# Feed-forward output tile 0 kept on chip, with its norm, residual sum and maxima formed inside the feed-forward stage

## The chip, the core and the metric

The kernel runs on one core of a Trainium2 chip. The core has five engines with queues of their own: TensorE (PE, matmuls; its weight loads are shown as PEld), VectorE (DVE), ScalarE (ACT), GpSimd (POOL) and SyncE (SP, which here only issues transfers). Each queue runs its instructions in order; semaphores order the queues against each other. Data live in SBUF (128 partitions), matmul results in PSUM, and everything larger in HBM behind 16 DMA engines. The metric is device time of one launch in microseconds (us), lower is better. Before the change it is 4735.76 us, the median of three runs (4731.34 to 4744.84).

## The reference

Four residual blocks work on one image tensor `x` of 4 batches, 384 channels and 64 x 64 pixels, each behind a norm over 32 groups of 12 channels (`_gn`). The change lies at the border of the last two: the end of block 2 (a gated channel mixer) and the beginning of block 3 (a 7x7 depthwise convolution with generated kernels).

```python
# block 2, its end (tok: tokens formed before; gate: one number per batch)
h1 = _gelu(_bn(_pw(tok, cm_w1), cm_g1, cm_b1))     # 384 -> 768 channels
h2 = _bn(_pw(h1, cm_w2), cm_g2, cm_b2)             # 768 -> 384; _bn: mean and variance over batches and pixels
ch = tok + h2
return gate * ch + (1.0 - gate) * x

# block 3, on _gn(x)
x_avg = x.mean(axis=(2, 3)); x_max = x.max(axis=(2, 3))
x_w = gelu(x_avg @ w_avg.T + b_avg + x_max @ w_max.T + b_max)
x_w = x_w[:, :, None] * w_mix[None, :, :]
kern = gamma * (xr * Nx) + beta          # xr: x_w as b x c x 7 x 7, Nx: its norm over the mean norm
out = depthwise_conv_7x7(x, kern)

# the whole: x = x + block(_gn(x)), for each of the four
```

## The kernel before

Channels lie on partitions in three tiles of 128, j = 0, 1, 2 (`NJ`), in an order that puts each group's channels together as far as possible; the rest of the groups is spread over the three tiles, so a group's mean (`of_groups`, one small matmul and a few copies) needs all three tiles. A batch of one tile is 128 x 4096 float32, 2 MB; work on it is done in quarters of 1024 pixels.

**The feed-forward stage, `phase_ef`.** Its first half (L1640 to L1692) makes the hidden layer and, beside it, everything of the block's output that doesn't need h2: `wx`, in HBM, with its sums per channel (`sums`). It uses the start of the strip buffer `self.z_` as a spare tile. The second half (L1702 to L1731) runs over batch b and quarter i. It loads a 3 MB block of the hidden layer (`f_h`, two buffers), applies a Gelu to each of its six parts (L1708), and for each output tile j forms two 512-pixel products of six matmuls each (L1720) into one of four PSUM tiles `h2_m`. ScalarE copies each to SBUF (L1727), VectorE takes its statistics (L1728), and a transfer from GpSimd's queue writes it to `self.h2` in HBM (L1729). A float32 matmul appears as two matmul instructions in the profile. After the last product, `over_batches` and `bn_scale_shift` (L1732) turn the statistics into a scale and shift, and L1736 to L1745 into `gh` and `g0` (h2's scale and shift, with the gate), `mean2` (the mean of the block's output, called x2) and `neg2`, for all three tiles.

**The convolution stage, `phase_g`.** It begins with loads of constants and gate weights, `group_means()` (which gives the group means `gm` and from them the offset `s_b`), and then, batch after batch for tile 0:

- `x2_of(0, b)`: x2 = wx + gh * h2 + g0, in quarters. h2 is loaded from HBM (L1963), scaled on GpSimd (L1965), added on VectorE (L1966), squared with a sum on ScalarE (L1976) and searched for its maximum on VectorE (L1977). The whole goes to HBM (L1979). wx of batches 0 to 2 was loaded ahead into the three tiles of `gx_tile` (`x2_ahead`); that of batch 3 and of all later calls is loaded when a tile is free again (L1957).
- `to_strips(0, b, x)`: subtracts the group mean (L1993), transposes on TensorE (L2003) and copies into the strip buffer as `z[:, channel, row pair, batch]`, on VectorE (L2008) or ScalarE (L2010). A strip copy so writes scattered single elements all over the buffer. `x2_of` of one batch and `to_strips` of the batch before alternate.

Then `conv7` runs over channels: a band matrix `toep` on VectorE or GpSimd (L2036) and products with the strips (L2049), for tile 0 first. Meanwhile `x2_of(1, b)` and `x2_of(2, b)` are worked off, a piece at a time; after these, `factors()` forms the gates, which need sums and maxima of all three tiles. `half_strips` and `boxes` serve the later tiles.

The order of the program isn't the order on the queues: a planner fixes each queue's order when the program is built, from the order in which operations are written, what each needs, and `tc.high_priority()`, which asks for an earlier place.

Of the kernel before, what the change touches and what calls it, by code (L numbers as in the profile page):

```python
# [21 lines left out]
F32 = mybir.dt.float32  # L22
# [6 lines left out]
NJ = 3  # L29
# [252 lines left out]
class _Builder:  # L282
# [1301 lines left out]
    def phase_ef(self, strips):  # L1584
        tc, nc = self.tc, self.nc
        with ExitStack() as ctx:
# [113 lines left out]
            st2 = cp.tile([P, NJ, B * 8, 6], F32, tag="h2_st", name="h2_st")  # L1700
            mvb = cp.tile([P, NJ, B, 2], F32, tag="h2_mvb", name="h2_mvb")
            for b in range(B):  # L1702
                for i in range(4):
                    blk = slice(i * 1024, (i + 1) * 1024)
                    h = hp.tile([P, 6, 1024], F32, tag="h", name="f_h")
                    nc.sync.dma_start(h, self.hidden[b][:, :, blk].rearrange("o p n -> p o n"))
                    for o in range(6):
                        last = nc.scalar.activation(  # L1708
                            h[:, o, :], h[:, o, :], AF.Gelu, bias=c1[:, o : o + 1], scale=a1[:, o : o + 1]
                        )  # L1710
                    if b == B - 1 and i == 3:
                        self.ln_exp(last)
                    if b == B - 1 and 0 < i:
                        nc.sync.dma_start(self.x2_ahead[i - 1], self.wx[i - 1][:, 0])
                    for j in range(NJ):
                        out = io.tile([P, 1024], F32, tag="x", name="f_h2")
                        for v in range(2):
                            m = self.pm("h2_m")
                            for o in range(6):
                                nc.tensor.matmul(  # L1720
                                    m,
                                    lhsT=w2[:, o, j * P : (j + 1) * P],
                                    rhs=h[:, o, v * 512 : (v + 1) * 512],
                                    start=o == 0,
                                    stop=o == 5,
                                )
                            nc.scalar.copy(out[:, v * 512 : (v + 1) * 512], m)  # L1727
                            nc.vector.bn_stats(st2[:, j, 8 * b + 2 * i + v, :], out[:, v * 512 : (v + 1) * 512])  # L1728
                        nc.gpsimd.dma_start(self.h2[b][:, j, blk], out)  # L1729
                for j in range(NJ):  # L1730
                    nc.vector.bn_aggr(mvb[:, j, b], st2[:, j, 8 * b : 8 * b + 8].rearrange("p a b -> p (a b)"))  # L1731
            a2, c2 = self.bn_scale_shift("bn_h2", *self.over_batches("h2", mvb), self.vec("cm_g2"), self.vec("cm_b2"))  # L1732


            self.mean2, self.neg2 = self.coef("mean2"), self.coef("neg2")
            nc.vector.tensor_reduce(self.mean2, sums, AX.X, ALU.add)  # L1736
            for j in range(NJ):
                nc.vector.tensor_scalar(self.gh[:, j, :], self.gate, a2[:, j : j + 1], None, ALU.mult)
                nc.vector.tensor_scalar(self.g0[:, j, :], self.gate, c2[:, j : j + 1], None, ALU.mult)
                m = self.mean2[:, j, :]  # L1740
                nc.vector.scalar_tensor_tensor(m, m, 1.0 / N, self.g0[:, j, :], ALU.mult, ALU.add)
                part = self.sm([P, B], "h2_part")
                nc.vector.tensor_mul(part, self.gh[:, j, :], mvb[:, j, :, 0])
                nc.vector.tensor_add(m, m, part)
                nc.vector.tensor_scalar(self.neg2[:, j, :], m, -1.0, None, ALU.mult)  # L1745


    def phase_g(self):
# [8 lines left out]
        with ExitStack() as ctx:  # L1757
# [31 lines left out]
            self.x2_var, self.x2_max = (cp.tile([P, NJ, B, 4], F32, tag=k, name=k) for k in ("x2_var", "x2_max"))  # L1789


            self.z = self.z_[:, 0 : P * 136].rearrange("p (c k b) -> p c k b", k=34, b=B)
            nc.gpsimd.memset(self.z_[:, P * 136 :], 0.0)
            nc.gpsimd.memset(self.z[:, :, 0], 0.0)
            self.group_means()
            behind = iter(())
            for b in range(B):
                for x in self.x2_of(0, b):
                    next(behind, None)
                for _ in behind:  # L1800
                    pass
                behind = self.to_strips(0, b, x)
            for _ in behind:
                pass
# [144 lines left out]
    def x2_of(self, j, b):  # L1949
# [3 lines left out]
        if self.x2_ahead:  # L1953
            x = self.x2_ahead.pop(0)
        else:
            x = self.gx_tile("x2")
            nc.sync.dma_start(x, self.wx[b][:, j])  # L1957
        for q in range(4):
            sl = slice(q * 1024, (q + 1) * 1024)

            pool, tag = (self.gt_p, "rest") if j == 0 and q % 2 else (self.gw_p, "w7")
            h = pool.tile([P, 1024], F32, tag=tag, name="g_h2", bufs=3)
            nc.sync.dma_start(h, self.h2[b][:, j, sl])  # L1963
            if j == 0:
                nc.gpsimd.tensor_scalar(h, h, at(self.gh), at(self.g0), ALU.mult, ALU.add)  # L1965
                nc.vector.tensor_add(x[:, sl], x[:, sl], h)  # L1966
            else:
                for v in range(2):
                    m = self.pm("x2_m")
# [221 lines left out]
```

## Time and profile before

| what | value |
|---|---|
| median of three runs | 4735.76 us |
| the profiled execution | 4751.16 us, its span 4749.0 us |
| PE, busy | 4376.2 us, 92% of the span |
| DVE, busy | 2851.0 us, 60% |
| ACT, busy | 1958.1 us, 41% |
| POOL, busy | 845.5 us, 18% |
| DMA | 745.55 MB, mean 157 GB/s |
| second half of the feed-forward stage | 3533 to 4031 us of the span |
| between its last product and the first 7x7 product | 4031 to 4110 us |
| first tile's 7x7 products, to the gates | 4110 to about 4330 us |

The profile is of one execution. Busy time of PE is counted from start to modelled end of matmuls that overlap, so a busy PE need not be at its peak. The row of slices gives busy shares in tenths of 40 equal slices of 118.7 us; slices 34 and 35 hold the border of the two stages:

```profile
PE   7899999999999999998978999699999999578889
DVE  6766566655556455555777888655521111767788
PEclk9999999999999999998989999799999999698999
DMA  4301211121112111112328999766764442997787
```

PEclk is the clock that TensorE was granted, in tenths of full speed.

### The profile page before, as it was taken

To read this page: it belongs to the slowest core of one execution; us is meant where nothing else is said; L and a number is where in the kernel's file an instruction comes from. 1 tells how busy PE (TensorE), PEld (TensorE's weight loads), DVE (VectorE), ACT (ScalarE), POOL (GpSimd) and SP (SyncE) were. 2 spreads that over 40 slices of the span, in tenths; PEclk is the share of its full clock that TensorE was granted. 3 is DMA by queue.
4 is the path that set the end of the run, shared out by engine and by line. 5 is a ranking of instruction groups with operands and counts; after the bars stand their busy time and mean duration, and the time that the engine had idled before them with its cause. 6 is when DMAs were issued, how large, how long until landed. Compare 5 with 4: busy or idle time off the path is not lost. (4 is left out here: it accounts for less than half of the span.)

```text
span 4749.0 us, 49714 instructions
## 1 busy us (share of the span) xinstructions
PE 4376.2 (92%) x18447; PEld 2434.2 (51%) x18447; DVE 2851.0 (60%) x4650; ACT 1958.1 (41%) x2904; POOL 845.5 (18%) x786
## 2 busy tenths in 40 slices
PE   7899999999999999998978999699999999578889
PEld 2233444344443444434448888344444444578889
DVE  6766566655556455555777888655521111767788
ACT  4444444444444444443525666311124332764321
POOL 1000000000000000000025666000000000436655
PEclk9999999999999999998989999799999999698999
DMA  4301211121112111112328999766764442997787
GB/s 142 108 33 54 91 60 67 47 81 34 60 67 68 49 34 67 67 40 88 111 81 289 327 337 324 276 257 252 258 236 159 159 151 111 360 346 228 234 271 257
DMA packets 286015, 745.55 MB, mean 157 GB/s; under 512 B 22491, under 2 KB 122950, under 8 KB 273734
## 3 DMA queue, kind: packets, MB, share of 16 engines
q1 hardware_dynamic: 212344, 414.77, 27.5%
q0 software_dynamic: 40464, 180.77, 10.1%
q10 hardware_dynamic: 32958, 146.75, 7.7%
q8 instruction: 149, 2.44, 0.2%
q14 instruction: 100, 0.82, 0.1%
HBM read 439.95 MB, written 302.25 MB: 156 GB/s over the span
## 5 line engine op out<-in xcount | busy, mean ns | idle before, releaser
L819 ACT ACTIVATE probs<-sc_s 128x1024 f32<-128x1024 f32 x512 | 496.5, 1019 | 697.2 <-PE av L929 597.5
L929 PE MATMUL av<-probs,vt 128*128 128x512 f32 x1536 | 721.8, 607 | 0.0
L1128 DVE SCALAR_TENSOR_TENSOR acc<-band,vecs,acc 128x512 f32<-128x512 f32 x708 | 494.6, 745 | 49.7 <-POOL band L1089 45.3
L1720 PE MATMUL h_m<-f_h,cm_w_t 128*128 128x512 f32 x1152 | 497.7, 595 | 7.4 <-ACT f_h L1708 7.4
L1418 PE MATMUL conv_m<-toep,z 128*128 128x192 f32 (+1 forms) x2304 | 446.9, 352 | 33.3 <-DVE z L1347 12.5
L929 PEld LDWEIGHTS av<-probs,vt 128*128 128x128 f32 x1536 | 278.0, 192 | 342.3 <-issue 338.6
L1418 PEld LDWEIGHTS conv_m<-toep,z 128*128 128x128 f32 x2304 | 403.3, 195 | 56.8 <-ACT d_o L1429 16.9
L2049 PE MATMUL conv_m<-toep,z 128*128 128x128 f32 x3072 | 395.4, 287 | 30.8 <-DVE toep L2036 19.5
L2049 PEld LDWEIGHTS conv_m<-toep,z 128*128 128x128 f32 x3072 | 381.4, 203 | 32.9 <-POOL toep L2036 10.2
L1664 PE MATMUL h_s<-e_tok,cm_w_t 128*128 128x512 f32 x768 | 363.3, 595 | 4.1 <-DVE e_tok L1649 4.1
L1720 PEld LDWEIGHTS h_m<-f_h,cm_w_t 128*128 128x128 f32 x1152 | 219.9, 191 | 285.3 <-issue 273.9
L1728 DVE BATCH_NORM_STATS2 h_st<-f_h 128x6 f32<-128x512 f32 x96 | 66.5, 694 | 430.2 <-ACT f_h L1727 430.2
L811 PE MATMUL sc_s<-q,k 32*128 32x512 f32 x2048 | 306.8, 643 | 15.3 <-ACT probs L819 15.1
L1399 POOL TENSOR_TENSOR toep<-w,band 128x1280 f32<-128x1280 f32 x94 | 272.5, 2899 | 179.2 <-PE conv_m L1418 179.2
L1051 PE MATMUL t_m<-w_in_t,xb 128*128 128x384 f32 x768 | 281.3, 502 | 3.1 <-DVE coef L1068 3.1
L965 PE MATMUL proj_m<-xm,w_proj_t 128*128 128x512 f32 x576 | 271.5, 611 | 6.3 <-DVE xm L904 4.9
L1671 ACT COPY e_h<-h_s 128x1024 f32<-128x1024 f32 x96 | 97.2, 1012 | 400.9 <-PE h_s L1664 400.9
L1673 DVE BATCH_NORM_STATS2 h_st<-e_h 128x6 f32<-128x512 f32 x192 | 123.5, 686 | 218.4 <-ACT e_h L1671 218.3
L1664 PEld LDWEIGHTS h_s<-e_tok,cm_w_t 128*128 128x128 f32 x768 | 146.7, 191 | 188.7 <-issue 184.1
L972 DVE SCALAR_TENSOR_TENSOR x_res<-proj_m,bn_c,x_res 128x512 f32<-128x512 f32 x96 | 71.8, 748 | 240.5 <-PE proj_m L965 240.4
L1051 PEld LDWEIGHTS t_m<-w_in_t,xb 128*128 128x128 f32 x768 | 143.4, 194 | 138.2 <-issue 58.4
L1664 PE MATMUL h_s<-z,cm_w_t 128*128 128x512 f32 x384 | 196.9, 595 | 0.0
(438 smaller groups left out, 6394.9 us busy)
## 6 DMA issues: line engine op xcount, KB each, us to landing
d<-d_o ACTq DMA_DIRECT2D x48, 1024.0 KB
c_d<-d SPq DMA_DIRECT2D x48, 1024.0 KB
hid<-e_h ACTq DMA_DIRECT2D x16, 3072.0 KB
f_h<-hid SPq DMA_DIRECT2D x16, 3072.0 KB
x_in<-in_x SPq DMA_DIRECT2D x96, 256.0 KB
x_res<-in_x SPq DMA_DIRECT2D x32, 768.0 KB
xa<-x_res POOLq DMA_DIRECT2D x32, 768.0 KB, 3.9
xa_out<-xa SPq DMA_DIRECT2D x32, 768.0 KB
```

Source lines behind the costliest of these rows:

```text
L811: nc.tensor.matmul(s[:, g], lhsT=k4[32 * g : 32 * g + 32, c], rhs=q[i][32 * g : 32 * g + 32], start=True, stop=True,)
L819: nc.scalar.activation(p[:, h * 1024 : (h + 1) * 1024], s[:, 2 * h : 2 * h + 2].rearrange("p a b -> p (a b)"), AF.Exp, scale=0.25,)
L929: nc.tensor.matmul(av[0], lhsT=vt[:, 4 * c + v, :], rhs=p[:, v * 512 : (v + 1) * 512], start=c == 0 and v == 0, stop=c == 7 and v == 3,)
L965: nc.tensor.matmul(m, lhsT=self.w_proj[:, j, o * P : (o + 1) * P], rhs=xm[:, j], start=j == 0, stop=j == NJ - 1,)
L1051: nc.tensor.matmul(m[:, 0:C], lhsT=xb[:, j], rhs=self.w_in[:, j, :], start=j == 0, stop=j == NJ - 1,)
L1128: nc.vector.scalar_tensor_tensor(out, src(j, k), w, done, ALU.mult, ALU.add)
L1399: eng.tensor_tensor(t, self.w53[:, at : at + 160].rearrange("p (m n) -> p m n", n=8).unsqueeze(2).to_broadcast([P, 20, 8, 8]), band.rearra ...
L1418: nc.tensor.matmul(m[:, c * 256 + to : c * 256 + to + 64 * (k1 - k0)], lhsT=self.z_[:, at : at + P], rhs=t[:, 10 * c + k0 : 10 * c + k1].r ...
L1664: nc.tensor.matmul(s[:, v, :], lhsT=w1[:, j, o * P : (o + 1) * P], rhs=t[j][:, v * 512 : (v + 1) * 512], start=j == 0, stop=j == NJ - 1,)
L1673: nc.vector.bn_stats(st[:, o, 8 * b + 2 * i + v, :], h[:, o, v * 512 : (v + 1) * 512])
L1720: nc.tensor.matmul(m, lhsT=w2[:, o, j * P : (j + 1) * P], rhs=h[:, o, v * 512 : (v + 1) * 512], start=o == 0, stop=o == 5,)
L2049: nc.tensor.matmul(m[:, ch % 4 * P : (ch % 4 + 1) * P], lhsT=self.z_[:, at : at + P], rhs=t[:, 8 * c + 2 * i : 8 * c + 2 * i + 2].rearrang ...
```

## The change

The 48 jobs (b, i, j) of the second half become a list, in which the last quarter's tile-0 job changes places with the job before it, so that three jobs of tiles 1 and 2 follow the last job of tile 0. Products of tile 0 are copied into `self.z_` at their batch and quarter, and are no longer written to HBM. After the last of them, `h2_norms` is done for tile 0 alone, and `x2_first()` yields the work of `x2_of(0, b)` in 32 pieces, batch 3 first; six pieces are written ahead of each of the last three jobs, the other 14 behind them and behind the norm of tiles 1 and 2. For batches 0 to 2 the sum lands in the tile that holds wx and the squares go over h2 in the strip buffer; for batch 3 wx comes in quarters and the sum stays in the strip buffer.

`phase_g` then has only `group_means()` and four calls of `to_strips`. That one now works in parts of 8, 8, 8, 8 and 1 row pairs instead of three of 11, with the scaling of two parts and the strip copies of five of nine PSUM tiles on VectorE. For batch 3, which lies in the strip buffer, all five parts are scaled out first; then the buffer's edges are cleared, and the transposes begin. `x2_of` keeps only its branch for tiles 1 and 2. The two-row `edge` tile of `boxes` moves to another pool.

```diff
+            self.x2_var, self.x2_max = (self.gx_p.tile([P, NJ, B, 4], F32, tag=k, name=k) for k in ("x2_var", "x2_max"))
+            jobs = [(b, i, j) for b in range(B) for i in range(4) for j in range(NJ)]
+            jobs[-4:-3], jobs[-3:-2] = jobs[-3:-2], jobs[-4:-3]
+            tiles, own = {}, iter(())
...
+            for b, i, j in jobs:
+                blk = slice(i * 1024, (i + 1) * 1024)
+                if j == 0:
                     h = hp.tile([P, 6, 1024], F32, tag="h", name="f_h")
+                    tiles[b, i] = h
...
-                    for j in range(NJ):
-                        out = io.tile([P, 1024], F32, tag="x", name="f_h2")
...
-                        nc.gpsimd.dma_start(self.h2[b][:, j, blk], out)
...
+                for _ in range(6):
+                    next(own, None)
+                self.feed_back(b, i, j, w2, tiles[b, i])
+                if (b, i, j) == (B - 1, 3, 0):
+                    self.h2_norms(slice(0, 1))
+                    own = self.x2_first()
+            with tc.high_priority():
+                self.h2_norms(slice(1, NJ))
+            for _ in own:
+                pass
+
+    def feed_back(self, b, i, j, w2, h):
...
+        at = b * N + i * 1024
+        out = self.io.tile([P, 1024], F32, tag="x", name="f_h2") if j else self.z_[:, at : at + 1024]
...
+        if j:
+            nc.gpsimd.dma_start(self.h2[b][:, j, i * 1024 : (i + 1) * 1024], out)
...
+    def x2_first(self):
+
+        nc = self.nc
+        spare = self.z_[:, B * N : B * N + 1024]
+        for b in (B - 1, 0, 1, 2):
+            at = lambda v: v[:, 0, b : b + 1]
+            for q in range(4):
+                sl = slice(q * 1024, (q + 1) * 1024)
+                h = self.z_[:, b * N + q * 1024 : b * N + q * 1024 + 1024]
+                if b == B - 1:
+                    x, junk = h, spare if q % 2 else self.io.tile([P, 1024], F32, tag="wx", name="f_wx", bufs=1)
+                    nc.sync.dma_start(junk, self.wx[b][:, 0, sl])
+                    other = junk
+                else:
+                    x, junk = self.x2_ahead[b][:, sl], h
+                    other = x
+                nc.gpsimd.tensor_scalar(h, h, at(self.gh), at(self.g0), ALU.mult, ALU.add)
+                nc.vector.tensor_add(x, other, h)
+                yield
+                nc.scalar.activation(junk, x, AF.Square, bias=at(self.neg2), accum_out=self.x2_var[:, 0, b, q : q + 1])
+                nc.vector.tensor_reduce(self.x2_max[:, 0, b, q : q + 1], x, AX.X, ALU.max)
+                yield
+            nc.gpsimd.dma_start(self.scratch["x2"][b][0], self.x2_tile(b))
...
-            nc.gpsimd.memset(self.z_[:, P * 136 :], 0.0)
-            nc.gpsimd.memset(self.z[:, :, 0], 0.0)
-            self.group_means()
-            behind = iter(())
-            for b in range(B):
-                for x in self.x2_of(0, b):
-                    next(behind, None)
...
-                behind = self.to_strips(0, b, x)
...
+            with tc.high_priority():
+                self.group_means()
+            self.to_strips(0, B - 1, self.x2_tile(B - 1), True)
+            for b in range(B - 1):
+                self.to_strips(0, b, self.x2_tile(b))
             self.pair_scales(1)
...
+    def to_strips(self, j, b, x, first=False):
...
+        def strips(k0, n, y):
+            for i in range(0, n, 4):
+                m = self.pm("strip_m")
+                w = min(n - i, 4)
+                for k in range(w):
+                    nc.tensor.transpose(m[:, k * P : (k + 1) * P], y[:, (i + k) * P : (i + k + 1) * P], self.ident)
+                mv = m.rearrange("p (k c) -> p k c", c=P)[:, 0:w, :]
+                at = 1 + k0 + i
+                zv = self.z[:, :, at : at + w, b]
+                if (k0 + i) % 8 == 0 and k0 + i < 32:
+                    nc.scalar.copy(zv, mv.rearrange("p k c -> p c k"))
+                else:
+                    nc.vector.tensor_copy(zv.rearrange("p c k -> p k c"), mv)
+
+        behind = []
+        for k0, n in ((0, 8), (8, 8), (16, 8), (24, 8), (32, 1)):
+            tag, bufs = ("y", 2) if k0 % 16 else ("rest", 3)
+            y = self.gt_p.tile([P, n * P], F32, tag=tag, name="ax2", bufs=bufs)
...
+            if k0 % 16:
+                nc.vector.tensor_scalar(to, src, s, o, ALU.mult, ALU.add)
+            else:
+                nc.scalar.activation(to, src, AF.Identity, bias=o, scale=s)
+            behind.append((k0, n, y))
+            if not first:
+                strips(*behind.pop())
+        if first:
+            nc.gpsimd.memset(self.z_[:, P * 136 :], 0.0)
+            nc.gpsimd.memset(self.z[:, :, 0], 0.0)
+        for p in behind:
+            strips(*p)
...
-                above = self.sm([P, 2, W], "edge")
+                above = self.gt_p.tile([P, 2, W], F32, tag="edge", name="edge", bufs=2)
```

The new `h2_norms(js)` holds the operations of L1732 to L1745 for the tiles it is given.

## The prediction

> **What bounds it now.** I read the row of slices first: PE falls to 5 tenths in one slice near the end, and its clock to 6. The chain of waits says why: PE sets the time until the last feed-forward product, and then nothing single does for 78.6 us, until the first 7x7 convolution product (by line, in order of time; start, us, what):
>
> ```profile
> 3533.62 497.74 PE h_m L1720 x1152
> 4031.38 0.59 ACT f_h L1727
> 4032.00 0.70 DVE h_st L1728
> ...
> 4034.88 0.21 ACT bn_h_a L374
> 4035.20 3.89 DMA g_h<-h
> 4039.10 6.88 DMA g_h<-h
> ...
> 4070.51 13.22 DMA g_h<-h
> ...
> 4109.97 12.55 PE conv_m L2049 x96
> ```
>
> I call the end of the products E = 4031.4. Busy time by stage (engine columns, then granted clock, DMA share, GB/s) shows what the stretch after E lacks:
>
> ```profile
> core 0: us, PE busy (x) PEld busy (x) DVE busy (x) ACT busy (x) POOL busy (x), PEclk, DMA share, GB/s
> 3533.00:4031.00 498.00, 497.38 (x1152) 219.86 (x1152) 69.86 (x106) 164.40 (x192) 24.99 (x47) 0.99 0.42 158
> 4031.00:4110.00 79.00, 32.50 (x136) 26.77 (x135) 61.62 (x91) 61.23 (x77) 38.32 (x43) 0.52 0.91 334
> 4110.00:4330.00 220.00, 177.90 (x1355) 174.44 (x1356) 159.92 (x200) 128.32 (x200) 95.43 (x87) 0.88 0.94 330
> ```
>
> Three things are to be seen. Before E only PE is full: VectorE is 14% busy, DMA 42%. After E the DMA engines are (91%), with VectorE and ScalarE close behind (78%). And the first 220 us of convolution are DMA-bound too (94% at 330 GB/s), so a gain in the gap is kept only if that traffic also starts earlier. The groups of the gap (busy, mean ns, idle before):
>
> ```profile
> L2003 PE MATMUL strip_m<-ident,ax 128*128 128x128 f32 x132 | 31.5, 425 | 38.3 <-ACT ax L1993 28.3 <-issue 3.5 <-ACT z L2010 3.0
> L1965 POOL TENSOR_SCALAR g_h<-g_h,gh,g 128x1024 f32<-128x1024 f32 x16 | 25.5, 1596 | 9.9 <-DMA g_h<-h 6.2 <-ACT z L2010 3.6
> L1966 DVE TENSOR_TENSOR x<-x,g_h 128x1024 f32<-128x1024 f32 x16 | 22.1, 1394 | 3.3 <-POOL g_h L1965 3.3
> L1977 DVE TENSOR_REDUCE x_max<-x 128x1 f32<-128x1024 f32 x16 | 18.9, 1198 | 0.0
> L1976 ACT ACTIVATE g_h<-x,neg 128x1024 f32<-128x1024 f32 x16 | 18.2, 1140 | 4.3 <-DVE x L1966 4.2
> L2008 DVE COPY z<-strip_m 128x512 f32<-128x512 f32 x12 | 13.0, 1084 | 8.6 <-PE strip_m L2003 8.6
> ```
>
> **The products, moved.** One job (i, j) is 497.74/48 = 10.37 us. With (3,0) of the last batch pulled ahead of (2,2), three jobs follow the last tile-0 product, which now ends at T0 = E - 31.1 = 4000.3. It starts at 3989.9, 10.4 us earlier than now. Its six Gelus (L1708) are done at 3989.8 and the first at 3983.6, so PE doesn't wait; 6.3 us of cover for the transfer in front of them. The outputs of tile 0 stay on chip: 16 writes of 512 KB leave the stage, where DMA isn't the limit: 0.
>
> **Norm of tile 0, early.** The same dozen small operations as now: from E to the last of gh and g0 for one tile, 4031.4 to about 4036.0, is 4.6 us. So they stand at 4004.9; one GpSimd scaling (1.19 us uncontended) and the first add starts at 4006.2. The second, split-off norm adds some 10 small VectorE operations of 0.17, 1.7 us; I count them below.
>
> **Adds, maxima and squares.** Same 16 quarters, no load before them. VectorE limits: 22.1 + 18.9 = 41.0 us busy, less 32 overlaps of 0.08 between neighbours in its timeline, 38.4. On top of it from 4006.2 on: six bn_stats at 0.69, 4.1; two aggregates 0.7; the second norm 2.5; group means and the small work of the next stage 2.2. Sum 47.9, so it ends at 4054.1, E + 22.7. Some 24 us of it lie beneath the last products. GpSimd's 16 scalings (25.5), the in-order ScalarE copies of the three jobs (six at 0.58) and the squares fit beside it. Behind a square that waits for its add stand the PSUM copies of the products; with four PSUM tiles PE has two jobs of cover, 20.7 us, so I cost that at 0 (up to 5 if the planned order is bad). SP's four wx loads for the last batch stand behind the last hidden load (issued 3969.6), with nothing but the next stage's loads behind them. GpSimd's queue also holds the h2 writes of tiles 1 and 2, which wait for those copies; a scaling queued behind one waits up to a few us, while VectorE still has a maximum to do.
>
> The cost unknown here is VectorE beside GpSimd. The row has adds at a mean of 1394 ns against 1202 at best: 3 us over all 16, already in the 41.0. [...] Were every add to wait for a whole scaling, that would be 16 x 1.19 = 19 us, 16 more than the row. I take the row[...].
>
> **Strips.** They can't start before the group means, which still need tiles 1 and 2 (about E + 9, hidden by the quarters). And because the outputs lie in the strip buffer itself, no strip may be written before every quarter's add and square is done, and batch 3 is scaled out of it. So what was interleaved is now in sequence; that is the price of the change. Two scalings move to VectorE at about 0.81 (the 128x1024 row below), then two memsets, here 0.6: first strip at E + 25. ScalarE from E: copy and norm 1.1, gate-weight transfers issued 6.0 (4037.0 to 4043.0), two table loads 2.6, seven squares 9.3, scalings 2.5: 21.5, just inside.
>
> ```profile
> L1677 DVE TENSOR_SCALAR e_x<-e_x,gx,gn x48: 743/809/815, 3020.3 to 3432.7; 128x1024 f32<-128x1024 f32 x48
> 4090.00:4100.00 10.00, 7.83 (x33) 6.00 (x31) 9.17 (x9) 9.92 (x13) 1.43 (x4) 0.50 0.95 354
> 4192.53 1.22 PE strip_m L1931 x11
> ```
>
> The 132 transposes remain. Now 11 take 2.61 us, 0.237 each; among convolution products, 11 take 1.22 (third line). Per batch, warm PE needs 3.7 us and cold 7.8, while ScalarE needs 4 copies at about 0.9 plus 2.5 of scaling, 6.1, and VectorE 4 at 0.93 plus 0.3 and 1.6, 5.6. So the clock decides which engine paces it. In the second line (4090 to 4100) PE was 78% busy with transposes and the clock stayed 0.50. [...] By the first: about 22 us for all strips, by the second 132 x 0.237 = 31.3. The row is with the second, and I take it. Three PSUM tiles of transposes (2.8) can stand ready before the first strip may be written, so 28.5, and 1.4 for the last copy and its signal: first convolution product at E + 55 = 4086. I add 2 us for ScalarE and VectorE not fitting perfectly: 4088, against 4110: **22 us gained**.
>
> **Does DMA let it be kept?** From 4031 to 4330 it moves 79 x 0.334 + 220 x 0.330 = 99.0 MB. Gone or moved before E: 16 reads of h2 (8.4), the wx of batch 3 (2.1), the x2 write of batch 3 (2.1). That leaves 86.4 MB, 261 us at 0.331. But the three tiles for tile 1's wx come free only as the strips of batches 0, 1, 2 are scaled out; I put the first at E + 39 (first strip E + 25, batch 3's 7.8, and most of batch 0's). Until then there are 9.7 MB to move, 29 us, so 10 us idle, and some 3 later. 274 us against 299: 25 gained. The present first load for tile 1 is at E + 52:
>
> ```profile
> 4083.49 0.32 SPq L1957 DMA_DIRECT2D x<-wx x1
> ```
>
> The smaller sum decides, so 22. The moved "edge" tile keeps its two buffers: 0. Against the profiled time, 4751.2 (span 4749.0 and 2.2 around it), that is 4729. That execution is 15.4 above the median of the runs, so the same gain from 4735.8 gives **4714**.
>
> **Rivals.**
> - Warm strips, 0.18. [...] Then ScalarE's 6.1 a batch paces it: first product at about E + 46, first load E + 35; gain 31, 4705. Against: the 0.50 row.
> - [...], 0.11. Up to 16 us later on the quarters; half of it or more leaves a gain of 6 to 14, about 4726. Against: the rows' 3 us.
> - It doesn't do what it says, 0.06. The order on a queue isn't program order now (a GpSimd "toep" of the later loop runs at 4049.6 amid the scalings). If the quarters fall behind E, VectorE ends at E + 48 and the strips at E + 78: no gain, 4735.
> - Late tiles, 0.07, slower. Every load for tile 1 waits for the strip phase, and the convolution behind it is DMA-bound: 261 us plus all idle time before. It decides once the first wx load for tile 1 is issued later than about E + 63, as 261 + 38 is the present 299. Strips held to E + 50, by quarters that run late, put it at E + 68: some 7 us slower, 4743. Against: it needs 25 us of delay beyond my sum.
>
> **Chances.** The forecast has 0.58, with its own range 4704 to 4722. A measurement tells about 0.3% here, 14 us, from no change. Nearly all of the forecast's share, the warm case and a little of the port case lie beyond it: faster 0.80. Within it: most of the port case, the case without effect, the forecast's tail and half of the late tiles: 0.14. Slower 0.06. The range takes in the warm case with extra traffic relief and most of the port case: 4698 to 4731.
>
> **What would show it.** Scalings and adds of tile 0 before E, the first near 4006; no load of h for tile 0; adds ending near E + 23; the first strip copy right behind them; PEclk 0.5 through the strips and 11 transposes in 2.6 us; the first convolution product near E + 57; a first wx load for tile 1 near E + 39; then a DMA share above 0.9 and about the same 220 us to the gates. I am wrong if PE stalls in its last three jobs, if strips are paced by copies, or if the convolution stage grows by what the gap lost.

## The result, and the profile after

The changed kernel takes 4721.1 us, the median of 13 runs (4709.16 to 4733.37), beside 4737.17 us for 13 runs of the kernel before (4724.88 to 4747.4). The ratio is 0.9969, with a 95% interval of 0.9957 to 0.9981: 14.7 us faster, 9 to 20 by the interval (the medians themselves lie 16.1 apart), where 22 were forecast. The profiled execution took 4721.1 us, its span 4719.3.

The two spans differ by 29.7 us, but 8.3 of these lie ahead of E, the end of the last feed-forward product: E is at 4023.1 after and at 4031.4 before. 7.4 of them are there already when the second half begins (3526.2 and 3533.6), in code that the change doesn't touch, and over all kernels of this study E lay between 4018 and 4040. So I compare distances from E. The chain of waits of the changed kernel, in its part behind E (start, us, what):

```profile
4087.10 10.97 PE conv_m L2099 x96
...
4276.44 6.16 PE xw_m L1920 x36
```

The first 7x7 product starts at 4087.10, E + 64.0, where it was E + 78.6: the gap is **14.6 us shorter**. The last gate product `xw_m` ends at 4282.6, E + 259.5, against E + 275.0. So the stage behind the gap kept its length, 195.5 us against 196.4, and the gap's gain is kept up to there. From the gates to the end the profiled execution is another 6 us shorter (436.7 for 442.6); one profile of each kernel can't tell whether the change did that. The changed kernel, busy time by stage and then by steps of the gap:

```profile
core 0: us, PE busy (x) PEld busy (x) DVE busy (x) ACT busy (x) POOL busy (x), PEclk, DMA share, GB/s
3525.00:4023.00 498.00, 496.81 (x1152) 219.63 (x1152) 92.44 (x135) 174.45 (x209) 37.22 (x46) 0.99 0.40 149
4023.00:4087.00 64.00, 22.34 (x135) 16.82 (x134) 52.78 (x88) 41.18 (x56) 17.19 (x30) 0.71 0.71 266
...
4087.00:4277.00 190.00, 147.97 (x1145) 144.49 (x1146) 139.93 (x164) 119.37 (x184) 75.00 (x61) 0.89 0.97 344
...
4046.00:4056.00 10.00, 0.57 (x2) 0.50 (x2) 5.15 (x31) 2.62 (x3) 5.80 (x11) 0.50 1.01 337
4056.00:4060.00 4.00, 2.60 (x12) 2.42 (x12) 0.53 (x1) 3.99 (x7) 1.25 (x3) 0.50 1.05 366
4060.00:4070.00 10.00, 8.11 (x48) 5.93 (x47) 9.02 (x11) 9.29 (x11) 2.71 (x3) 0.84 0.29 95
4070.00:4080.00 10.00, 6.65 (x48) 4.84 (x45) 9.56 (x12) 9.03 (x11) 0.80 (x4) 1.00 0.84 334
```

VectorE's work ahead of E grew from 69.9 to 92.4 us and PE still is full there: the moved work lies beneath the products. The gap now has DMA at 71% instead of 91%, and the stage behind it is full of transfers again (97%). Two rows speak against the forecast. From 4046 to 4056 VectorE and ScalarE are half and three quarters idle: the gap has a hole. And in the strips PE's clock goes to 0.84 and 1.00, not 0.50. The groups of the moved work, from 3990 to the first 7x7 product (busy, mean ns, idle before):

```profile
L1794 POOL TENSOR_SCALAR z<-z,gh,g 128x1024 f32<-128x1024 f32 x16 | 24.1, 1513 | 12.7 <-DVE g L1770 12.6
...
L1795 DVE TENSOR_TENSOR x<-x,z 128x1024 f32<-128x1024 f32 x12 | 18.5, 1559 | 0.5 <-POOL z L1794 0.5
...
L1798 DVE TENSOR_REDUCE x_max<-x 128x1 f32<-128x1024 f32 x12 | 14.2, 1193 | 0.0
```

The quarters' scalings and maxima cost what they did (24.1 us against 25.5, a mean of 1193 ns against 1198); the adds of batches 0 to 2 are dearer, 1559 ns against 1394. The strips, in the same view:

```profile
L2030 PE MATMUL strip_m<-ident,ax 128*128 128x128 f32 x132 | 21.6, 308 | 15.6 <-DMA a_pair<-s_s 8.7 <-ACT z L2035 5.5 <-DVE z L2037 1.2
L2035 ACT COPY z<-strip_m 128x512 f32<-128x512 f32 x16 | 17.5, 1137 | 3.4 <-PE strip_m L2030 3.3
...
L2037 DVE COPY z<-strip_m 128x512 f32<-128x512 f32 x16 | 17.3, 1092 | 6.5 <-PE strip_m L2030 6.3
```

The transposes' 31.5 us are 21.6, and what PE waits for in between are the copies (5.5 + 1.2) that free its PSUM tiles. The hole shows in VectorE's timeline (start, us, what; `h_m` and `h_d` are the norm of tiles 1 and 2):

```profile
4033.50 0.68 DVE L1750 BATCH_NORM_STATS2 h_st<-f_h 128x6 f32<-128x512 f32 x1
...
4035.22 0.36 DVE L1754 BATCH_NORM_AGGREGATE h_mvb<-h_st 128x2 f32<-128x48 f32 x1
...
4036.58 0.14 DVE L393 TENSOR_REDUCE h_m<-h_mvb 128x2 f32<-128x8 f32 x1
4036.64 1.21 DVE L1795 TENSOR_TENSOR x<-x,z 128x1024 f32<-128x1024 f32 x1
4037.77 0.16 DVE L394 TENSOR_SCALAR h_m<-h_m 128x2 f32<-128x2 f32 x1
4037.84 1.21 DVE L1795 TENSOR_TENSOR x<-x,z 128x1024 f32<-128x1024 f32 x1
4038.98 0.15 DVE L396 TENSOR_TENSOR h_d<-h_mvb,h_m 128x8 f32<-128x8 f32 x1
...
4043.87 2.33 DVE L1798 TENSOR_REDUCE x_max<-x 128x1 f32<-128x1024 f32 x2
...
4049.34 0.17 DVE L1893 COPY gm<-g_pg 128x12 f32<-128x12 f32 x1
...
4053.36 0.23 DVE L1831 COPY band_p<-band 128x64 f32<-128x64 f32 x1 [3.14 <-DMA band<-in_consts]
```

The quarters are done at 4046.2, E + 23.1. The norm in the kernel before (all three tiles at once), with nothing else on VectorE:

```profile
4033.13 0.17 DVE L393 TENSOR_REDUCE h_m<-h_mvb 128x3 f32<-128x12 f32 x1
...
4039.41 0.17 DVE L1844 COPY gm<-g_pg 128x12 f32<-128x12 f32 x1
```

There it began at E + 1.8 and reached the group means 6.3 us later. Now it is late and slow. Late: it begins at 4036.58, E + 13.5, as the last product's statistics (4033.50) and their sum (4035.22) come only then. Slow: as long as there are quarters, each of its small operations, of some 0.15 us, stands behind one or two of their 1.2 us operations, so the chain to the group means takes 12.8 us, from 4036.58 to 4049.34. And what follows waits again, for a constant. ScalarE's timeline, its queue of transfers included (ACTq):

```profile
4029.64 0.56 ACT L1749 COPY f_h<-h_m 128x512 f32<-128x512 f32 x1
...
4047.53 0.37 ACTq L1824 DMA_DIRECT2D w_gate<-in_w_avg_t  x1
...
4052.88 0.44 ACTq L1824 DMA_DIRECT2D w_gate<-in_w_max_t  x1
4053.35 1.28 ACT L1838 ACT_TABLE_LOAD   x1 [7.78 <-DMA mean<-in_consts]
...
4054.87 1.28 ACT L343 ACT_TABLE_LOAD   x1
4056.16 2.65 ACT L2053 ACTIVATE ax<-z,s_b,s_s 128x960 f32<-128x960 f32 x3
...
4058.96 1.10 ACT L2035 COPY z<-strip_m 128x512 f32<-128x512 f32 x1
```

The first line is the last product's copy out of PSUM, 6.5 us behind E: it stands behind squares, which wait for VectorE's adds. The gate weights, forecast at E + 6, are asked for at 4047.53, E + 24.4, when the second norm is done. Then come two table loads, three scalings, and at last the first strip copy: E + 35.8, 11 us later than forecast.

### The profile page after: what moved, and what is told of

It reads as the page before. It is cut to its first block, busy times and chain, and to the rows that moved or that the text cites. A ratio compares the mean times of both kernels' runs of the same rounds, so it can differ in the third digit from the quotient of the medians.

```text
span 4719.3 us, 49674 instructions
## 1 busy us (share of the span) xinstructions
PE 4351.5 (92%) x18447; PEld 2414.3 (51%) x18447; DVE 2867.2 (61%) x4677; ACT 1948.0 (41%) x2898; POOL 836.7 (18%) x770
## 5 line engine op out<-in xcount | busy, mean ns | idle before, releaser
L2099 PEld LDWEIGHTS conv_m<-toep,z 128*128 128x128 f32 x3072 | 377.9, 202 | 36.2 <-POOL toep L2086 12.8
L811 PE MATMUL sc_s<-q,k 32*128 32x512 f32 x2048 | 306.3, 641 | 15.4 <-ACT probs L819 15.2
L1750 DVE BATCH_NORM_STATS2 h_st<-f_h 128x6 f32<-128x512 f32 x64 | 44.1, 692 | 260.1 <-ACT f_h L1749 260.1
```

The lines of the kernel that those rows point to most:

```text
L811: nc.tensor.matmul(s[:, g], lhsT=k4[32 * g : 32 * g + 32, c], rhs=q[i][32 * g : 32 * g + 32], start=True, stop=True,)
L2099: nc.tensor.matmul(m[:, ch % 4 * P : (ch % 4 + 1) * P], lhsT=self.z_[:, at : at + P], rhs=t[:, 8 * c + 2 * i : 8 * c + 2 * i + 2].rearrang ...
```

## Experiments

My theory after this: the forecast mechanism holds, and 7 us of it are lost because norm, group means, constants and table loads stand one behind the other between the quarters and the strips. Rivals: it is the quarters that set the strips' start anyway; the overlap with the products gains nothing and only the saved traffic counts; the pace of the strips sets the gap. Every kernel starts from the changed one. Times are in us behind each kernel's own E; the ratio is to the kernel before on the same chip, with its 95% interval.

| kernel | quarters end | first strip copy | first 7x7 product | gates' product ends | span ends | median | ratio |
|---|---|---|---|---|---|---|---|
| before | - | - | 78.6 | 275.0 | 717.6 | 4737.2 | 1 |
| changed | 23.1 | 35.8 | 64.0 | 259.5 | 696.2 | 4721.1 | 0.9969 (0.9957 to 0.9981) |
| e1 norm ahead | 28.2 | 30.4 | 61.4 | 257.1 | 692.9 | 4715.3 | 0.9953 (0.9935 to 0.9971) |
| e2 no tables | 23.0 | 33.4 | 61.9 | 261.1 | 692.1 | 4712.8 | 0.9959 (0.9942 to 0.9976) |
| e3 no swap | 34.2 | 38.2 | 69.6 | 263.6 | 709.1 | 4723.0 | 0.9978 (0.9969 to 0.9987) |
| e4 late quarters | 49.2 | 51.4 | 82.9 | 276.7 | 718.4 | 4733.0 | 0.9995 (0.9981 to 1.0008) |
| e5 = e1 + e2 | 28.2 | 30.2 | 59.8 | 252.5 | 693.0 | 4711.6 | 0.9955 (0.9938 to 0.9973) |
| e6 = e5, scaling on ScalarE | 26.5 | 28.0 | 54.7 | 253.5 | 689.4 | 4710.9 | 0.9949 (0.9932 to 0.9966) |
| e7 = e5, six PSUM tiles | 28.2 | 30.3 | 52.7 | 245.0 | 694.0 | 4707.3 | 0.9942 (0.9922 to 0.9961) |
| e8 more reads | 23.0 | 35.8 | 64.5 | 268.7 | 704.6 | 4725.9 | 0.9989 (0.9979 to 1.0) |
| e9 = e6 + e7 | 26.9 | 28.4 | 52.6 | 248.6 | 694.0 | 4709.1 | 0.9945 (0.9927 to 0.9964) |
| e10 six PSUM tiles alone | 23.1 | 35.8 | 61.5 | 258.1 | 700.3 | 4717.3 | 0.9964 (0.9953 to 0.9975) |
| e11 = e9, four jobs behind tile 0 | 15.6 | 17.6 | 43.1 | 237.3 | 678.8 | 4711.2 | 0.995 (0.993 to 0.9969) |

The intervals are some 9 to 18 us wide. A step of a few us is read from the distances, each from one profiled execution; the medians only say whether they go the same way. From the gates to the end of the span it takes between 431.0 (e2) and 449.0 us (e7), without an order that follows the experiments: what of a gain at the gates reaches the end isn't shown by one profile each.

**e1: the norm of tiles 1 and 2 ahead of the remaining quarters.** `h2_norms` returns its last instruction.

```diff
             with tc.high_priority():
-                self.h2_norms(slice(1, NJ))
-            for _ in own:
-                pass
+                behind = self.h2_norms(slice(1, NJ))
+            with tc.issue_after(behind.ins):
+                for _ in own:
+                    pass
```

> E is the end of the last feed-forward product; in the changed kernel the first strip copy stands at E + 35.8 and the first convolution product at E + 64.0, though the last quarter of tile 0 ends at E + 23. Chain theory: the strips are late because the second norm's small operations each stand behind a quarter's operation on VectorE, and everything of the next stage (gate weights, constants, two table loads, group means) waits for that norm. With the seven remaining quarters queued behind the norm, the first strip copy comes to E + 25 to 27, the first product to E + 54 to 56, the time falls by some 9 us against the changed kernel (ratio to before about 0.995). Throughput rival: VectorE and ScalarE have the same work either way and the strips wait for the last quarter, which now ends some 4 us later; first product not before E + 61, ratio 0.997 as the changed kernel.

The chain is gone: the small matmul of the group means is at 4038.20, E + 11.2, and the gate weights are asked for at E + 10.9. But the gap is only 2.6 us shorter. PE's timeline and then VectorE's, of this kernel:

```profile
3979.58 47.37 PE L1743 MATMUL h_m<-f_h,cm_w_t 128*128 128x512 f32 x110
4038.20 0.57 PE L419 MATMUL g_pg<-mean,group 128*128 128x12 f32 x2 [11.25 <-DVE neg L1777]
```

```profile
4052.82 2.33 DVE L1800 TENSOR_REDUCE x_max<-x 128x1 f32<-128x1024 f32 x2
...
4056.36 0.80 DVE L2053 TENSOR_SCALAR ax<-z,s_s,s_b 128x1024 f32<-128x1024 f32 x1
...
4057.36 1.08 DVE L2039 COPY z<-strip_m 128x512 f32<-128x512 f32 x1
```

The quarters, which stood aside for the norm, now end 5.1 us later (4055.15, E + 28.2), and the first copy is right behind them. Theory and rival each hold half: between the quarters' end and the first copy there were 12.7 us and are now 2.2, but half of that went into quarters that end later. Another 2.8 us went into the strips, 31.0 us instead of 28.1, at whose start ScalarE has a table load (4056.70). Undoing one wait gave the next one.

**e2: the square root by logarithm and exponential**, so that no table of activations is changed there.

```diff
-            self.ln_exp(nc.scalar.activation(self.mix2, self.mix2, AF.Sqrt))
+            nc.scalar.activation(self.mix2, self.mix2, AF.Ln)
+            nc.scalar.activation(self.mix2, self.mix2, AF.Exp, scale=0.5)
```

> The square root of the mixing weights' norm is formed as exp(0.5 ln), so that two table loads (2.6 us together) leave ScalarE's queue between the gate weights' transfers and the first scaling for the strips. Chain theory: they lie on the path, first strip copy 2.6 us earlier (about E + 33), first product E + 61.4. Rival (VectorE's scalings, which wait for the constants' transfer, set the first strip): no more than 1 us earlier, E + 63 or later. The time alone can't tell 2.6 us from noise of some 5; the trace can.

The first copy is 2.4 us earlier and the gap 2.1 shorter, about the two loads of 1.28: in the changed kernel they stand bare on the path. The gates come no earlier (261.1 against 259.5).

**e3: the order of jobs as before**, so that two products' jobs follow tile 0's last instead of three.

```diff
-            jobs[-4:-3], jobs[-3:-2] = jobs[-3:-2], jobs[-4:-3]
```

> Tile 0's last job keeps its old place, so two jobs (20.7 us) instead of three (31.1) cover the quarters. Cover theory: the quarters end 10.4 us later after E (E + 33 instead of E + 23), the first strip at about E + 45, the first product at E + 73 to 75, time within 0.1% of before plus or minus 5 us. Rival: the gain comes from h2 of tile 0 staying on chip (8.4 MB of reads less), not from the cover; first product within 3 us of E + 64.

The quarters end 11.1 us later, about the one job (10.37) that no longer covers them. The gap grows by only 5.6, since the wait behind the quarters shrinks from 12.7 to 4.0: in this order most of the chain runs beside the quarters.

**e4: no quarter ahead of the end.** The pieces are all written behind the jobs and behind the norm of all three tiles; tile 0 still stays on chip.

```diff
-                for _ in range(6):
-                    next(own, None)
...
-                if (b, i, j) == (B - 1, 3, 0):
-                    self.h2_norms(slice(0, 1))
-                    own = self.x2_first()
             with tc.high_priority():
-                self.h2_norms(slice(1, NJ))
-            for _ in own:
-                pass
+                behind = self.h2_norms(slice(0, NJ))
+            with tc.issue_after(behind.ins):
+                for _ in self.x2_first():
+                    pass
```

> Tile 0 stays in the strip buffer, but none of its adds, squares and maxima stand ahead of the end of the products: one norm for all three tiles, then 16 quarters on VectorE. Cover theory: first add at E + 7, 38.4 us of quarters, so E + 46 and the first strip at about E + 48, as group means, gate weights and table loads are hidden by then; first product about E + 76, time within 5 us of before. Rival (less DMA traffic pays): first product at E + 68 or earlier, since the quarters no longer wait for loads, and ratio to before 0.998 or less.

The gap is 82.9, the time that of the kernel before. Sixteen reads of 512 KB less don't make up for it that strips now follow the quarters, where they alternated. Against e1, which has the same reads, the same sequence and likewise the norm ahead, the gap is 21.5 us longer: **what shortens the gap is the overlap with the last products.**

**e5: e1 and e2 together.**

> The norm ahead of the last seven quarters, and no table loads. With the norm ahead, the last quarter on VectorE ended at E + 28 and the first two strip copies stood at E + 30.4 and 31.0, the ScalarE one right behind a table load; first product E + 61.4. Throughput theory (after the norm is out of the way, the quarters on VectorE set the strips): the table loads end beside them, so at most 1.5 us earlier, first product about E + 60, time within 2 us of either part alone. Chain theory (each part was on the path): the two savings of 2.6 and 2.1 us add up, first product at E + 59 or earlier.

The first product is at E + 59.8: 4.2 us gained of the 4.7 that the two gave apart, and what the throughput theory said. The first copy comes no earlier than in e1; what e2 adds lies within the strips, where ScalarE now has no table loads (in e1 they ran at 4054.20 and 4056.70).

**e6: e5, and the scaling of a quarter on ScalarE instead of GpSimd.**

```diff
-                nc.gpsimd.tensor_scalar(h, h, at(self.gh), at(self.g0), ALU.mult, ALU.add)
+                nc.scalar.activation(h, h, AF.Identity, bias=at(self.g0), scale=at(self.gh))
```

> As the kernel with norm ahead and no table loads, and the 16 scalings of h2 on ScalarE in place of GpSimd. Port theory: the adds average 1.55 us beside GpSimd's scalings (one took 4.1 us through three of them) against 1.22 alone; without GpSimd they fall to 1.22 to 1.25 and the quarters on VectorE end some 5 us earlier, at E + 23 to 24, the first product at E + 55 to 57. Rival (ScalarE takes the place): 16 scalings at 1.14 us and the PSUM copies queue up on ScalarE, which then delays adds or the last products; quarters end no earlier than E + 27, or PE stalls before E.

Adds now take 1.21 to 1.23 us each, but the quarters end only 1.7 us earlier than in e5, not 5: VectorE now waits for ScalarE, 1.72 us for the last product's copy and 1.59 us for a step of the norm, which stand behind scalings there. The rival holds half. In the changed kernel the 16 adds took 24.8 us, 1.55 on average (the 12 shown above 18.5, the four of batch 3 another 3.4 + 2.9). The longest one there, in VectorE's timeline and beside it GpSimd's:

```profile
4013.74 4.10 DVE L1795 TENSOR_TENSOR x<-x,z 128x1024 f32<-128x1024 f32 x1
```

```profile
4013.22 3.55 POOL L1794 TENSOR_SCALAR z<-z,gh,g 128x1024 f32<-128x1024 f32 x3
```

The add began while three scalings ran one behind the other, and ended about a microsecond behind the last of them: one add's length. Elsewhere there, two adds that began beside a scaling took 3.62 us (from 4024.84, the scalings until 4026.25), two with none beside them 2.34 (from 4031.23). Over all 16, adds beside scalings cost 24.8 - 16 x 1.22 = 5.3 us more, not the 19 of a wait for a scaling at every add. The first copy is 2.2 us earlier, and the strips are 2.8 us shorter, 26.7 instead of 29.5; I didn't find what in them became shorter. At the gates nothing of it is seen (253.5 against 252.5).

**e7: e5, and six PSUM tiles for the transposes instead of three**, the other three lent by the `c` tiles.

```diff
-                m = self.pm("strip_m")
+                if i % 8:
+                    m = self.psum.tile([P, 512], F32, tag="c", name="strip_c", bufs=3)
+                else:
+                    m = self.pm("strip_m")
```

> As the kernel with norm ahead and no table loads, and every other strip tile comes from the three PSUM tiles of the later convolution, so six instead of three. Buffer theory: the strips pace at 7.0 us a batch because ScalarE and TensorE wait for each other through three tiles (ScalarE idle some 0.6 us twice a batch); with six, ScalarE's busy time sets it, 6.2 us a batch, and the strip phase shrinks from about 30 to 26 or 27 us. Copy theory: the copies themselves (1.1 us each, in order) set the pace; less than 1 us gained.

The strips, from first copy to first product, take 22.5 us instead of 29.5, and the median is the lowest of the study. The copies' groups in e5, then in e7:

```profile
L2038 ACT COPY z<-strip_m 128x512 f32<-128x512 f32 x16 | 17.6, 1131 | 6.6 <-PE strip_m L2033 6.3 <-DVE ax L2054 0.3
...
L2040 DVE COPY z<-strip_m 128x512 f32<-128x512 f32 x16 | 16.8, 1088 | 3.7 <-PE strip_m L2033 3.6
```

```profile
L2043 DVE COPY z<-strip_c 128x512 f32<-128x512 f32 x16 | 16.9, 1119 | 0.7 <-PE strip_c L2036 0.6
...
L2041 ACT COPY z<-strip_m 128x512 f32<-128x512 f32 x16 | 16.6, 1160 | 0.3 <-DVE ax L2057 0.3
```

The copies take as long as ever; what went is their idle time before, 10.3 us on the two engines against 1.0. With three tiles PE waited for a copy to free a tile (8.0 us for ScalarE's copies in e5, 2.0 in e7) and the next copy waited for PE (6.3 and 3.6 us in e5, as above). (Nearly all of VectorE's copies now come from tiles of their own, too; that the number does it, and not this, isn't tested.) The gates come 7.5 us earlier than in e5, but at the end of the span nothing of it is seen (694.0 against 693.0).

**e8: the traffic given back.** 16 loads of 512 KB ahead of the strips, whose data nothing uses.

```diff
+            for b in range(B):
+                for q in range(4):
+                    h = self.gw_p.tile([P, 1024], F32, tag="w7", name="more", bufs=3)
+                    nc.sync.dma_start(h, self.h2[b][:, 1, q * 1024 : (q + 1) * 1024])
             self.to_strips(0, B - 1, self.x2_tile(B - 1), True)
```

> The changed kernel, with 16 extra reads of 512 KB from h2 (tile 1) into the three buffers that the old loads of tile 0 used, ahead of the strips; nothing uses them. DMA theory: the border and the stage behind it are DMA-bound as a whole, so the 8.4 MB that the change took away are worth up to 24 us less what is idle in the gap; the time rises by 8 us or more. Gap theory: what was gained is VectorE's and ScalarE's work moved under the products; the extra reads run in DMA time that is otherwise idle in the gap, the first product stays within 1 us of E + 64 and the time rises by less than 4 us.

The gap is the same, 64.5, but the stage behind is 8.7 us longer (204.2 against 195.5), and the ratio 0.0020 higher, against some 9 us of the distance. In SyncE's timeline of this kernel the loads for tile 1 begin behind the added ones, at E + 56.7 instead of E + 44.0:

```profile
4054.35 29.33 SPq L1854 DMA_DIRECT2D more<-h  x16
4083.79 0.37 SPq L2007 DMA_DIRECT2D x<-wx  x1
```

The 8.4 MB would be 24 us at the stage's 344 GB/s; by that estimate some 15 cost no time. The traces show a place for part of them: in the ten microseconds from E + 35 the DMA share is 0.94 at 328 GB/s, where the changed kernel has 0.30 at 106, and over the 29 us from there to the first product 9.3 MB are moved for its 7.4. So each theory holds half: the first product stays, and the reads, placed here, give back behind the gap more than half of what it gained.

**e9: e6 and e7 together**, to see whether their gains add up.

> Norm ahead, no table loads, six PSUM tiles for the strips, and the scalings on ScalarE. Of these, six tiles took the first product from E + 59.8 to E + 52.7 and the scalings on ScalarE alone from E + 59.8 to E + 54.7. Theory (two separate limits, quarters on VectorE and then strips): both add, first product at E + 47 to 48.5, and from E to the gates about 240 us against 245 with six tiles alone. Rival (the convolution stage behind is DMA-bound and gives an earlier start back): first product as said, but E to the gates 243 us or more and the time as with six tiles alone.

They don't: E + 52.6 against 52.7 in e7. The first copy comes 1.9 us earlier and the strips are 1.7 us longer. In e7 the two copying engines were full already (VectorE 22.3 and ScalarE 22.7 us busy in the 23 from 4053 to 4076), so there is little left to gain in the strips but by fewer or shorter copies.

**e10: six PSUM tiles in the changed kernel, nothing else.**

> The changed kernel with nothing but six PSUM tiles for the strips. Buffer theory: its strip phase shrinks from 28 us to 22 or 23, the first product comes to E + 58 to 59 and the time falls by 4 to 6 us. Rival (six tiles help only where the first batch's scalings are already done, as with the norm ahead): less than 3 us.

Strips of 25.7 us instead of 28.1, a gap of 61.5 instead of 64.0. Behind the chain of norm and table loads they are worth a third of the 7.1 us that they bring in e7, less than the 3 us of the rival. It fits that PE waits here 1.00, 1.71 and 2.35 us for VectorE's scalings within the strips, in e7 never over 0.7; no run tests that alone.

**e11: e9, and one more job behind tile 0's last.**

```diff
-            jobs[-4:-3], jobs[-3:-2] = jobs[-3:-2], jobs[-4:-3]
+            jobs.insert(len(jobs) - 5, jobs.pop(-3))
```

> As the one with norm ahead, no table loads, six tiles and scalings on ScalarE, and tile 0's last job yet one place further ahead, so that four jobs (41.5 us) follow it. Cover theory: quarters start 10.4 us earlier, but the last hidden block's first Gelu (4 us after the job could start, by the present trace) holds PE 4 to 7 us; first product at E + 38 to 41, of which the stall is to be taken off: net 3 to 6 us faster than without. Rival: the six Gelus and the stall take it all, and PE stands still 10 us or more ahead of E; no gain or slower.

The gap falls to 43.1, 9.5 less than in e9, for a stall of PE of 3.36 us ahead of the job that was moved, as PE's timeline shows (its input waits for its Gelu). The two products behind the stall take 12.3 us (3983.33 to 3995.63, when ScalarE copies the second out of PSUM), where two took 10.3 ahead of it (copies 5.15 apart, at 3974.86 and 3980.01). So the second half takes 5.4 us longer than in e9 (503.0 and 497.7):

```profile
3983.33 53.46 PE L1743 MATMUL h_m<-f_h,cm_w_t 128*128 128x512 f32 x120 [3.36 <-ACT f_h L1716]
...
4079.85 17.65 PE L2105 MATMUL conv_m<-toep,z 128*128 128x128 f32 x144 [1.68 <-DVE z L2043]
```

The first 7x7 product is at 4079.85, and the gates come 11.3 us earlier behind E, 6 with those 5.4 set against it; the span ends 15.2 earlier, 10 net. The median, 4711.2 against 4709.1, doesn't show it, and intervals of 18 us can't tell; I leave it open.

The lowest median is e7's: 4707.31 us, 0.9942 (0.9922 to 0.9961) of the kernel before, against 0.9969 (0.9957 to 0.9981) for the changed one. The intervals overlap by a little, and those of e1, e2, e5, e6, e9 and e11 by more than half of their width. Its distance to the gates is 14.5 us shorter than the changed kernel's, but of these only 2.2 are left at the end of its span. That it is faster than the changed kernel is likely, not shown.

## Why the prediction was right, point by point

- **Products and first norm.** Right: PE shows no wait in its last three jobs; the first add starts at 3998.10, E - 25.0, where 4006.2, E - 25.2, was forecast.
- **Adds, maxima, squares.** Right in sum, E + 23.1 for E + 22.7, in part by luck: adds beside GpSimd cost 24.8 us and not 22.1, and VectorE stood idle for 1.6, but of the 4.7 us of small operations that I had counted in, only about 1 ran before the quarters' end. Single adds are longer beside scalings (4.10 us the longest, 1.21 to 1.23 in e6), but a scaling each, 19 us, isn't paid. The maxima are no longer for it: one took 1.16 us at 4023.76, beside three scalings that ran from 4022.70 to 4026.25.
- **The step that failed**: "group means, which still need tiles 1 and 2 (about E + 9, hidden by the quarters)", and with it "first strip at E + 25". I counted the small operations only as VectorE's time and let them be done when their inputs were. Two terms were put at nothing. The norm began at E + 13.5 instead of E + 1.8, 11.7 us late: the last product's copy stands behind a square, a wait of which I wrote "I cost that at 0", since PE has tiles to go on with. PE did go on, but the norm waits for that copy, and its statistics stand behind quarters besides. And the chain took 12.8 us for 6.3: its dependent operations of some 0.15 us, on a queue full of 1.2 us ones, paid one or two of these at each link as long as there were quarters. The group means came at E + 26.2, and constants, gate weights and table loads, which I had beside the quarters ("21.5, just inside"), came behind them: first strip at E + 35.8. e1, e2 and e5 show it: without chain and tables it is E + 30.2 (e5). The other 5 us to E + 25 were never to be had in this way, since the norm, put ahead, delays the quarters by as much.
- **Strips.** The sum was near, 28.1 us for 28.5 + 1.4 (+ 2 for poor fitting), but by luck, for the reason was wrong: what I had named as a sign of being wrong, strips paced by copies, came true. I let PE at a clock of 0.50 set the pace; the clock rose to 1.00 and 16 copies on each engine through three PSUM tiles set it (e7: 22.5 with six). The rival "warm strips" was right on the clock, and its pace of about 22 us is what six tiles give; it missed the tiles. Of the prediction's two sums for all strips, about 22 us, with ScalarE as the pace, is for PE at 1.22 us for 11 transposes, 31.3 for PE at 2.61; that the 0.50 of the kernel before would hold here too was my estimate from its row, 4090 to 4100.
- **Is it kept?** Right: the stage behind keeps its length at a DMA share of 0.97. The first load for tile 1 came at E + 44.0 for the forecast E + 39, far from the E + 63 from which, by the prediction's estimate, late tiles would have cost time; SyncE's timeline of the changed kernel:

```profile
4067.15 14.45 SPq L2003 DMA_DIRECT2D x<-wx  x3
```

- **A wait for a scaling at every add** (the rival of 0.11, in its chances the port case) would have been as near to the measured time (4726 for 4721, the forecast 4714), but isn't the reason: 5.3 us of it are there, 3 of them in the sum already. **No effect** and **late tiles** didn't occur; e4 shows the first as it would look, in the time and in the gap.

In sum, 78.6 - 64.0 = 14.6 us of gap instead of 22: + 11 at the first strip, - 4 on strips with their margin. The measured 14.7 us agree with it. So the mechanism, work moved beneath the products, was right; that the sum came this near is in part luck, since the strips' wrong reason took off 4 of the 11 us.

## What to carry to other kernels

Where work is moved beneath a stage that one engine bounds, the gain is what fits beneath it (here 21.5 us of gap, e4 against e1): move the dependent tail first, and place the short chain that releases the next stage (a norm, its constants, its table loads) ahead of the long operations in the queue, since behind them its links here paid a whole one each (12.8 us for 6.3). Also ask what that chain's first input stands behind. Then ask what comes last behind it, for here taking away the chain, a wait of over 10 us, won 2.6 before the quarters held up the strips. In a pipeline of PE into copies, see whether the copying engines stand idle for want of PSUM tiles (here 10.3 us with three, 1.0 with six) before putting its pace down to PE's clock.

## What the runs showed of the hardware

In the changed kernel the strips, where PE has nothing but float32 transposes, were granted the full clock: 0.84 from 4060 to 4070 and 1.00 from 4070 to 4080, with PE 81% and 67% busy. In the kernel before, the same transposes at 78% busy, between 4090 and 4100, had 0.50. PE's timeline: the longest run of transposes without a wait in the kernel before, then the first run in the changed one:

```profile
4092.89 2.84 PE L2003 MATMUL strip_m<-ident,ax 128*128 128x128 f32 x11 [0.63 <-DVE z L2008]
```

```profile
4057.41 6.99 PE L2030 MATMUL strip_m<-ident,ax 128*128 128x128 f32 x32 [8.69 <-DMA a_pair<-s_s]
```

There the clock rose during that run: 0.50 up to 4063, 0.86 in the next microsecond, then 1.00 to the end of the strips, through waits of up to 0.9 us. In every experiment too the strips came to 1.00; in e8 the mean was 1.00 from 4072 to 4082 and 0.81 from 4082 to 4091, in e11 0.83 from 4060 to 4070 and 1.00 from 4070 to 4079. The length of the unbroken runs goes with it, but it doesn't settle it: in e1 the mean of 0.63 from 4057 to 4067, with 1.00 behind it, puts the rise near 4064.4 (an estimate), at the end of a run of 3.80 us from 4060.87; in e4 one of 3.86 us from 4076.62 passed at 0.50 (4073 to 4083). No run changed this alone, so the cause stays open.
